# Gates of a graph-and-convolution GRU layer: Sigmoid written as Tanh of the half, and the state's part of the new gate halved by ScalarE in PSUM

## The chip, the cores and the metric

The kernel runs on one core of a Trainium2 chip. A core has five engines that run side by side, each with its own instruction stream: TensorE (PE, matmuls into PSUM), VectorE (DVE, elementwise work), ScalarE (ACT, activation functions), GpSimd (POOL) and SyncE (SP); DMA queues move data between the device memory and the on-chip memory SBUF. The metric is the device time of one launch in microseconds (us), given as the median of several executions. One further execution was recorded by the hardware profiler; its rows are what this document reads.

## The reference

For each of 32 batch items with 512 nodes and 256 channels, the layer normalises `x`, takes the positive part, and feeds a GRU cell with two inputs: a convolution branch and a sum over neighbours weighted by `exp(-dist) * adj`.

```python
h = jnp.maximum(_layernorm(x, axis=-1), 0.0)
# inside the layer, x is h:
x_conv = relu(bn2(conv1d_17(relu(bn1(conv1d_1(xT))))) + xT).T
A = jnp.exp(-dist) * mask                     # dist from a 3-wide projection of x
x_nmp = jnp.einsum('bnm,bmd->bnd', A, relu(x @ w_msg.T + b_msg))
gi = jnp.concatenate([x_conv, x_nmp], axis=-1) @ w_ih.T + b_ih
gh = x @ w_hh.T + b_hh
r = jax.nn.sigmoid(gi_r + gh_r)
z = jax.nn.sigmoid(gi_z + gh_z)
nn_ = jnp.tanh(gi_n + r * gh_n)
out = x_outer + (1.0 - z) * nn_ + z * x
```

All of it is in float32.

## The kernel before, in words

The program has five streams, each a Python generator: `rows` (first convolution, 1 tap), `begins` (normalising and turning the items), `graphs` (messages, distances, Exp, mask, neighbour sums), `conv` (the 17-tap convolution as a fast algorithm with 25 products in each of seven groups of items) and `gates` (the GRU). A planner at the end of the file picks the next piece of the stream that lags most. It keeps an estimate `now` of TensorE's time and estimates `free` of when VectorE and ScalarE will have done what they were given. Work that depends on another engine's result isn't issued at once: `later(t, f)` queues the function `f` for the estimated time `t`, and `fill()` issues what is due after each piece and then gives VectorE background work. So each engine has a fixed order in the built program, and a change of what is issued also shifts the plan of everything else. The estimates know a fixed cost and a cost per element for each instruction; they don't know loads of activation tables.

**The gates.** For each item `b` there are two halves `o` of 128 output channels. Each of the tiles below is 128 channels by 512 nodes and fills one PSUM bank. The tiles come in turn from the pool `acc`, which has two buffers (L98), so a tile takes the bank of the tile before last, and its first matmul waits until that one has been read.

- `ps_r` gets six matmuls: two from the state `hTb`, two from `xconv`, two from `xnb`. `reset` (L1088) settles everything that is queued and applies Sigmoid with the summed bias `brz`; the result is `r`.
- `ps_h` gets two matmuls from the state. For o = 0 they stand between the first two and the last four matmuls of `ps_r`; for o = 1 they follow `ps_r`; for the very last half they follow `ps_z`. `reset_hidden` (L1096) makes `r = (ps_h + b_hh) * r` on VectorE in one operation.
- `ps_z` gets six matmuls; `update` (L1102) makes `z` by Sigmoid.
- `ps_n` gets four matmuls from `xconv` and `xnb`. `mix` (L1108) adds `ps_n` to `r` on VectorE, `mix_next` (L1035) applies Tanh on ScalarE, `mix_last` (L1042) forms `n + z * (h - n)` with three VectorE operations, and `leave` turns the tile, adds the residual `res`, and has it stored by GpSimd's queue.
- For the very last half, `mix_ahead` (L1065) prepares `z * h` plus the residual and `1 - z` ahead of time, and `ps_n` is made in two slices of 384 and 128 nodes.

The bank order is ps_r, ps_h, ps_z, ps_n, again and again: ps_z waits for the activation that reads ps_r, and ps_n waits for reset_hidden, which reads ps_h.

**Other users of ScalarE.** `kernel_exp` (L861) applies Exp to four tiles for each item; Copy, Identity and Relu evacuate the products of the other streams (`mid`, `h`, `right`, `part`, `msg`). In the program built from this kernel an activation table is loaded at the start and then at each change from Sigmoid to Exp and back, 52 loads in all.

All the instructions that the planner records for VectorE and ScalarE carry the line of its helper (L127), and nearly all matmuls carry L136, so the rows of the profile are told apart by tile names.

Of the kernel before, what the change touches and what calls it, by code (L numbers as in the profile page):

```python
# [8 lines left out]
F32 = mybir.dt.float32  # L9
AF = mybir.ActivationFunctionType  # L10
ALU = mybir.AluOpType
PSUM = bass.MemoryType.PSUM

P = 128
# [10 lines left out]
_COL = {}  # L25
# [23 lines left out]
def kernel(  # L49
# [34 lines left out]
    ND = D // P  # L84
# [8 lines left out]
    const = ctx.enter_context(tc.tile_pool(name="const", bufs=1))  # L93
# [37 lines left out]
    dve, act = Engine(nc.vector, 0.12, 0.00108), Engine(nc.scalar, 0.16, 0.0009)  # L131

    def matmul(ps, lhsT, rhs, **more):
        nonlocal now
        now += max(0.223, 0.005 + elements(ps) / 600.0)
        nc.tensor.matmul(ps, lhsT, rhs, **more)  # L136
# [21 lines left out]
    def later(t, f):  # L158
        LATER.append((t, f))
        LATER.sort(key=lambda e: e[0])  # L160
# [59 lines left out]
    def load_gates(b):  # L220
        if b >= B or b in HB:
            return
        settle_stores()
        HB[b] = late.tile([P, ND, N], F32, name="hTb", bufs=2)
        nc.sync.dma_start(HB[b], HD[b])
# [29 lines left out]
    vec = const.tile([P, _NCOL], F32)  # L255
# [747 lines left out]
    def gates(b):  # L1003

        load_gates(b)
        load_sums(b, 0)
        load_sums(b, 1)
        if b == 0:
            yield now + 8.0
        hT = HB[b]  # L1010
        x_in = []

        def cols(o, g):
            return slice(g * D + o * P, g * D + (o + 1) * P)

        def products(ps, o, g, ks, then=None, of=None):


            sources = ((whh, 0), (wih, 0), (wih, ND))
            of = of or ks  # L1020
            for k in ks:
                w, at = sources[k]
                for i in range(ND):
                    matmul(
                        ps, w[:, at + i, cols(o, g)], hT[:, i, :] if k == 0 else x_in[2 * k - 2 + i],
                        start=(k == of[0] and i == 0), stop=(k == of[-1] and i == ND - 1),
                    )
                if k == ks[-1] and then is not None:
                    then()
                if k == 2 and o == ND - 1 and g == 2:  # L1030
                    load_sums(b + 1, 0)
                    load_sums(b + 1, 1)
                yield now

        def mix_next(r, z, o, s):  # L1035
            act.activation(
                r[:, s], r[:, s], AF.Tanh,
                bias=vec[:, _COL["b_ih"] + 2 * ND + o : _COL["b_ih"] + 2 * ND + o + 1],
            )
            later(act.free + 0.3, lambda: mix_last(r, z, o, s))  # L1040

        def mix_last(r, z, o, s):  # L1042
            y = XR[b, o]
            if is_last(o):
                dve.tensor_tensor(z[:, s], z[:, s], r[:, s], op=ALU.mult)
                dve.transpose(r[:, s], z[:, s])
                dve.tensor_tensor(y[:, s], r[:, s], y[:, s], op=ALU.add)
                later(dve.free + 0.4, lambda: store(y, o, s))
                return
            t = late.tile([P, N], F32, name="o_sb")  # L1050
            dve.tensor_tensor(t, hT[:, o, :], r, op=ALU.subtract)
            dve.tensor_tensor(t, z, t, op=ALU.mult)
            dve.tensor_tensor(r, r, t, op=ALU.add)
            later(dve.free, lambda: leave(r, t, y, o))

        def leave(r, t, y, o):

            dve.transpose(t, r)
            dve.tensor_tensor(y, t, y, op=ALU.add)
            later(dve.free + 0.4, lambda: store(y, o, slice(0, N)))  # L1060

        def is_last(o):
            return b == B - 1 and o == ND - 1

        def mix_ahead(z, o):  # L1065

            y = XR[b, o]
            zh, turned = (late.tile([P, Q * U], F32, name="part", bufs=3)[:, :N] for _ in range(2))
            dve.tensor_tensor(zh, z, hT[:, o, :], op=ALU.mult)
            dve.tensor_scalar(z, z, -1.0, 1.0, op0=ALU.mult, op1=ALU.add)  # L1070
            dve.transpose(turned, zh)
            dve.tensor_tensor(y, turned, y, op=ALU.add)

        def store(y, o, s):
            for g in range(P // 32):
                at = slice(32 * g, 32 * g + 32)
                queue = nc.gpsimd if s.stop - s.start == N else nc.scalar if g % 2 else nc.sync
                queue.dma_start(  # L1078
                    OB[b][:, s.start // 32 : s.stop // 32, o * P + 32 * g : o * P + 32 * g + 32],
                    y[at, s].rearrange("i (k j) -> i k j", j=32),  # L1080
                )
            if s.stop == N:
                del XR[b, o]

        for o in range(ND):
            r = z = None

            def reset():  # L1088
                nonlocal r
                settle()  # L1090
                if b == o == 0:
                    load_res(b, o)
                r = late.tile([P, N], F32, name="r", bufs=2)
                act.activation(r, ps_r, AF.Sigmoid, bias=brz[:, o : o + 1])

            def reset_hidden(ps_h):  # L1096
                dve.scalar_tensor_tensor(
                    r, ps_h, vec[:, _COL["b_hh"] + 2 * ND + o : _COL["b_hh"] + 2 * ND + o + 1], r,
                    op0=ALU.add, op1=ALU.mult,
                )  # L1100

            def update():  # L1102
                nonlocal z
                load_res(b + o, 1 - o)
                z = late.tile([P, N], F32, name="z")
                act.activation(z, ps_z, AF.Sigmoid, bias=brz[:, ND + o : ND + o + 1])

            def mix(s=slice(0, N)):  # L1108
                dve.tensor_tensor(r[:, s], ps_n[:, s], r[:, s], op=ALU.add)
                later(dve.free + 0.3, lambda r=r, z=z, o=o: mix_next(r, z, o, s))  # L1110

            ps_r = acc.tile([P, N], F32, name="ps_acc")
            ps_h = None
            yield from products(ps_r, o, 0, (0,), of=(0, 2))
            if o == 0:
                ps_h = acc.tile([P, N], F32, name="ps_acc")
                yield from products(ps_h, o, 2, (0,))
                if b not in XC:
                    yield lambda: b in evacuated
                    yield evacuated[b]  # L1120
                    load_conv(b)
                if b not in RES:
                    yield XC_AT[b]
                    residual(b)
                yield lambda: RES[b] < 1e9
                yield RES[b]
                x_in.extend([XC[b][:, i, :] for i in range(ND)] + [XN[b, d] for d in range(ND)])
            yield from products(ps_r, o, 0, (1, 2), reset, (0, 2))

            def hidden():  # L1130
                ps = acc.tile([P, N], F32, name="ps_acc")
                yield from products(ps, o, 2, (0,), lambda: reset_hidden(ps))

            if ps_h is not None:
                reset_hidden(ps_h)
            elif not is_last(o):
                yield from hidden()
            ps_z = acc.tile([P, N], F32, name="ps_acc")
            yield from products(ps_z, o, 1, (0, 1, 2), update)
            if is_last(o):  # L1140
                later(act.free + 0.2, lambda: mix_ahead(z, o))
                yield from hidden()
            if o == 0:
                load_gates(b + 1)
                load_conv(b + 1)
            else:
                residual(b + 1)
            ps_n = acc.tile([P, N], F32, name="ps_acc")
            if b < B - 1 or o < ND - 1:
                yield from products(ps_n, o, 2, (1, 2) if o == 0 else (2, 1), mix)  # L1150
                continue

            for s in (slice(0, N - P), slice(N - P, N)):
                if s.start > 0:
                    ps_n = acc.tile([P, N], F32, name="ps_acc")
                for j in range(2 * ND):
                    matmul(
                        ps_n[:, s], wih[:, j, cols(o, 2)], x_in[j][:, s],
                        start=(j == 0), stop=(j == 2 * ND - 1),
                    )  # L1160
                mix(s)
                yield now
            settle()
# [102 lines left out]
    while 0 in NORMS:  # L1266
# [5 lines left out]
    brz = const.tile([P, 2 * ND], F32)  # L1272
    dve.tensor_tensor(
        brz, vec[:, _COL["b_ih"] : _COL["b_ih"] + 2 * ND], vec[:, _COL["b_hh"] : _COL["b_hh"] + 2 * ND],
        op=ALU.add,
    )
    NORM_AT[0] = act.free + LAG
    load(1)
    spare = cv.tile([P, 9 * NZ], F32, name="y")
# [88 lines left out]
```

## Time and profile before

| | before |
|---|---|
| median of 8 runs | 2113.61 us (2109.25 to 2118.49) |
| profiled execution, own time | 2116.55 us |
| its span, first to last instruction | 2114.6 us |
| mean granted clock of TensorE | 0.993 |
| GpSimd (POOL) busy | 339.7 us, 16% |
| table loads on ScalarE | 52, together 66.7 us |
| Sigmoid of r, of z | 64 of 687 ns, 64 of 688 ns |
| Tanh of the new gate, 128x512 | 63 of 718 ns |
| first gate matmul | about 240 us into the span |
| only gate work left from | about 1891 us, 31.94 us for each item |

In a group's row, "x64 | 44.0, 688 | 234.8 <-PE ps_acc" means 64 instructions, 44.0 us busy in all, 688 ns each on average, and 234.8 us in which the engine was idle just before them, ended mostly by TensorE's work on ps_acc. A float32 matmul of 128x512 appears as two records; eight records back to back take 3.43 us. In a row of the timeline the first number is the start in us from the beginning of the span, the second the duration, and a bracket gives the idle time before it and what ended it. A row of busy time by stretch gives the stretch, its length, the busy time and number of instructions of the five columns PE, PEld (weight loads), DVE, ACT and POOL, and then TensorE's granted clock, the DMA share and GB/s.

### The profile page before, as it was taken

To read this page: it belongs to the slowest core of one execution; us is meant where nothing else is said; L and a number is where in the kernel's file an instruction comes from. 1 tells how busy PE (TensorE), PEld (TensorE's weight loads), DVE (VectorE), ACT (ScalarE), POOL (GpSimd) and SP (SyncE) were. 2 spreads that over 40 slices of the span, in tenths; PEclk is the share of its full clock that TensorE was granted. 3 is DMA by queue.
4 is the path that set the end of the run, shared out by engine and by line. 5 is a ranking of instruction groups with operands and counts; after the bars stand their busy time and mean duration, and the time that the engine had idled before them with its cause. 6 is when DMAs were issued, how large, how long until landed. Compare 5 with 4: busy or idle time off the path is not lost.

```text
span 2114.6 us, 25916 instructions
## 1 busy us (share of the span) xinstructions
PE 2060.5 (97%) x8774; PEld 1260.1 (60%) x8774; DVE 1512.8 (72%) x2660; ACT 754.5 (36%) x1267; POOL 339.7 (16%) x582
## 2 busy tenths in 40 slices
PE   9999899999999999999999999999999999999998
PEld 5887466665666556656466665456665666654443
DVE  6887488985988668877497865588985877753333
ACT  5543532236432253322443323533124432232111
POOL 2000112211201021111121101211111110112111
PEclk9999999999999999999999999999999999999999
DMA  7446787776866767666766777677766656624332
GB/s 275 164 143 204 254 249 199 194 212 173 236 209 191 220 180 198 182 186 189 220 182 173 189 203 186 188 184 207 211 180 191 188 153 168 169 72 108 86 90 40
DMA packets 546436, 383.07 MB, mean 181 GB/s; under 512 B 456576, under 2 KB 473472, under 8 KB 545664
## 3 DMA queue, kind: packets, MB, share of 16 engines
q1 hardware_dynamic: 512992, 282.17, 50.6%
q0 software_dynamic: 28624, 86.01, 12.0%
q10 hardware_dynamic: 4688, 13.24, 1.6%
q8 instruction: 70, 1.15, 0.2%
q14 instruction: 62, 0.51, 0.1%
HBM read 281.95 MB, written 99.35 MB: 180 GB/s over the span
## 4 chain that ended last, share of the span: by engine, by line
PE 61%; DMA 2%; DVE 1%; issue 1%; ACT 1%; SPq 1%; POOL 0%; DVEq 0%; POOLq 0%; ACTq 0%
PE ps_acc L136 36%; PE ps_g L136 11%; PE ps_c L136 9%; PE ps_b L136 4%; PE ps_b L867 1%; DMA m_sb<-in_adj_dram 1%; ACT r L127 1%; PE ps_g L141 0%; DMA hd<-hT 0%; SPq L339 0%; DMA hT<-hd 0%; DVE y L127 0%; DMA xnb<-nd 0%; DVE right L127 0%; DVE at L127 0%
## 5 line engine op out<-in xcount | busy, mean ns | idle before, releaser
L136 PE MATMUL ps_acc<-hTb,whh 128*128 128x512 f32 x768 | 358.8, 598 | 18.9 <-ACT r L127 15.1
L136 PE MATMUL ps_acc<-xconv,wih 128*128 128x512 f32 (+1 forms) x772 | 362.3, 592 | 0.1
L136 PE MATMUL ps_acc<-xnb,wih 128*128 128x512 f32 (+1 forms) x772 | 358.6, 591 | 2.6 <-DMA xnb<-nd 2.6
L136 PEld LDWEIGHTS ps_c<-xd,w 128*128 128x128 f32 x2400 | 294.1, 191 | 33.0 <-issue 29.2
L136 PE MATMUL ps_c<-xd,w 128*128 128x135 f32 (+1 forms) x2400 | 303.5, 279 | 2.1 <-issue 2.1
L1078 POOL DMA_DIRECT2D out_dram<-res x252 | 164.5, 659 | 617.8 <-DVE res L127 527.0
L136 PEld LDWEIGHTS ps_acc<-hTb,whh 128*128 128x128 f32 x768 | 140.2, 190 | 180.1 <-issue 136.9
L136 PEld LDWEIGHTS ps_acc<-xnb,wih 128*128 128x128 f32 x772 | 142.7, 190 | 160.3 <-issue 153.0
L136 PEld LDWEIGHTS ps_acc<-xconv,wih 128*128 128x128 f32 x772 | 142.8, 190 | 157.5 <-issue 154.2
L136 PE MATMUL ps_g<-at,msg 128*128 128x512 f32 x512 | 227.2, 593 | 1.5 <-DVE at L127 1.5
L136 PEld LDWEIGHTS ps_b<-x,w 128*128 128x128 f32 x1200 | 157.0, 190 | 43.7 <-issue 37.3
L127 ACT ACTIVATE mid<-ps_b 128x270 f32<-128x270 f32 (+1 forms) x150 | 59.5, 396 | 343.9 <-PE ps_b L136 333.3
L127 DVE TENSOR_TENSOR r<-ps_acc,r 128x512 f32<-128x512 f32 (+1 forms) x65 | 44.2, 682 | 191.0 <-PE ps_acc L136 190.9
L136 PE MATMUL ps_b<-x,w 128*128 128x135 f32 (+1 forms) x1200 | 163.1, 278 | 1.1 <-DVE xd L127 1.1
L136 PEld LDWEIGHTS ps_g<-at,msg 128*128 128x128 f32 x512 | 95.4, 190 | 112.4 <-issue 108.1
L127 DVE SCALAR_TENSOR_TENSOR x<-x,x 128x544 f32<-128x544 f32 (+5 forms) x161 | 137.7, 855 | 2.9
L136 PE MATMUL ps_g<-hT,w 128*128 128x512 f32 (+4 forms) x288 | 124.4, 580 | 13.6 <-DMA hT<-hd 9.6
L127 DVE TENSOR_TENSOR msg<-ps_g,bmsg 128x256 f32<-128x256 f32 x128 | 53.8, 421 | 108.6 <-PE ps_g L136 108.3
L127 ACT ACTIVATE z<-ps_acc,brz 128x512 f32<-128x512 f32 x64 | 44.0, 688 | 234.8 <-PE ps_acc L136 234.7
L127 DVE TENSOR_TENSOR x<-x 128x272 f32<-128x272 f32 (+5 forms) x280 | 127.6, 497 | 0.2
L127 DVE TENSOR_TENSOR xd<-x 128x544 f32<-128x544 f32 (+1 forms) x150 | 106.6, 718 | 25.0 <-PE ps_c L136 24.7
L136 PE MATMUL ps_g<-wmsg,hTg 128*128 128x259 f32 x496 | 124.1, 382 | 0.3 <-DVE aug L127 0.3
(121 smaller groups left out, 2593.8 us busy)
## 6 DMA issues: line engine op xcount, KB each, us to landing
w<-wd SPq DMA_DIRECT2D x125, 768.0 KB, 5.4
m_sb<-in_adj_dram SPq DMA_DIRECT2D x384, 64.0 KB, 3.3
hd<-hT POOLq DMA_DIRECT2D x32, 512.0 KB, 6.6
hT<-hd SPq DMA_DIRECT2D x32, 512.0 KB, 4.8
hTb<-hd SPq DMA_DIRECT2D x32, 512.0 KB, 5.5
xnb<-nd SPq DMA_DIRECT2D x64, 256.0 KB, 3.6
xconv<-cd SPq DMA_DIRECT2D x32, 512.0 KB, 5.5
res<-in_x_dram SPq DMA_DIRECT2D x256, 64.0 KB, 3.1
```

Of the source, the lines that this page charges most:

```text
L127: getattr(self.engine, name)(*tiles, **more)
L136: nc.tensor.matmul(ps, lhsT, rhs, **more)
L867: nc.tensor.matmul(pss[c], gr.left[k, :], gr.right[k, :], start=True, stop=True, tile_position=(32 * c, 0),)
L1078: queue.dma_start(OB[b][:, s.start // 32 : s.stop // 32, o * P + 32 * g : o * P + 32 * g + 32], y[at, s].rearrange("i (k j) -> i k j", j=32),)
```

## The change

The gates no longer use Sigmoid. With t = tanh(a / 2), the sigmoid of a is (t + 1) / 2. `reset` and `update` apply Tanh with scale 0.5 and a bias that was halved once at the start (one more VectorE operation on `brz`, and one that makes the halved `bn` from `b_hh`). The factors 1/2 and the additions of 1 go into the operations that use r and z:

- the state's part of the new gate is halved, with its bias, by a new ScalarE activation `hidden_half`, which reads the bank of ps_h and writes the result back to the same bank; `reset_hidden` is then `(t_r + 1) * half` and is no longer issued directly after the matmuls or the activation of r but queued by `reset_later` for 0.3 us after the estimated end of ScalarE's work (and made at the latest in `mix`);
- in `mix_last` two of the three operations become operations with a constant: `(t_z + 1) * (h - n)` and `0.5 * that + n`;
- `mix_ahead` gets the same treatment.

```diff
-            dve.tensor_tensor(t, z, t, op=ALU.mult)
-            dve.tensor_tensor(r, r, t, op=ALU.add)
+            dve.scalar_tensor_tensor(t, z, 1.0, t, op0=ALU.add, op1=ALU.mult)
+            dve.scalar_tensor_tensor(r, t, 0.5, r, op0=ALU.mult, op1=ALU.add)
...
-            dve.tensor_tensor(zh, z, hT[:, o, :], op=ALU.mult)
-            dve.tensor_scalar(z, z, -1.0, 1.0, op0=ALU.mult, op1=ALU.add)
+            dve.scalar_tensor_tensor(zh, z, 1.0, hT[:, o, :], op0=ALU.add, op1=ALU.mult)
+            dve.tensor_scalar(z, z, -0.5, 0.5, op0=ALU.mult, op1=ALU.add)
             dve.transpose(turned, zh)
-            dve.tensor_tensor(y, turned, y, op=ALU.add)
+            dve.scalar_tensor_tensor(y, turned, 0.5, y, op0=ALU.mult, op1=ALU.add)
...
-                act.activation(r, ps_r, AF.Sigmoid, bias=brz[:, o : o + 1])
-
-            def reset_hidden(ps_h):
-                dve.scalar_tensor_tensor(
-                    r, ps_h, vec[:, _COL["b_hh"] + 2 * ND + o : _COL["b_hh"] + 2 * ND + o + 1], r,
-                    op0=ALU.add, op1=ALU.mult,
-                )
+                act.activation(r, ps_r, AF.Tanh, bias=brz[:, o : o + 1], scale=0.5)
+
+            def hidden_half(ps_h):
+                act.activation(ps_h, ps_h, AF.Identity, bias=bn[:, o : o + 1], scale=0.5)
+
+            halves = []
+
+            def reset_hidden():
+                if halves:
+                    dve.scalar_tensor_tensor(r, r, 1.0, halves.pop(), op0=ALU.add, op1=ALU.mult)
+
+            def reset_later(ps_h):
+                halves.append(ps_h)
+                later(act.free + 0.3, reset_hidden)
...
-                act.activation(z, ps_z, AF.Sigmoid, bias=brz[:, ND + o : ND + o + 1])
+                act.activation(
+                    z, ps_z, AF.Tanh, bias=brz[:, ND + o : ND + o + 1], scale=0.5
+                )

             def mix(s=slice(0, N)):
+                reset_hidden()
...
-                yield from products(ps_h, o, 2, (0,))
+                yield from products(ps_h, o, 2, (0,), lambda: hidden_half(ps_h))
...
-                yield from products(ps, o, 2, (0,), lambda: reset_hidden(ps))
+                yield from products(ps, o, 2, (0,), lambda: hidden_half(ps))
+                reset_later(ps)

             if ps_h is not None:
-                reset_hidden(ps_h)
+                reset_later(ps_h)
...
+    dve.tensor_scalar(brz, brz, 0.5, None, op0=ALU.mult)
+    bn = const.tile([P, ND], F32)
+    dve.tensor_scalar(
+        bn, vec[:, _COL["b_hh"] + 2 * ND : _COL["b_hh"] + 3 * ND], 0.5, None, op0=ALU.mult
+    )
```

## The prediction

> **What bounds the kernel now.** I read the busy table first, then who waited for whom, then the gaps of TensorE in order of time, then the groups of ScalarE.
>
> ```profile
> PE 2060.5 (97%) x8774; PEld 1260.1 (60%) x8774; DVE 1512.8 (72%) x2660; ACT 754.5 (36%) x1267; POOL 339.7 (16%) x582
> PE 61%; DMA 2%; DVE 1%; issue 1%; ACT 1%; SPq 1%; POOL 0%; DVEq 0%; POOLq 0%; ACTq 0%
> ```
>
> TensorE is busy for 2060.5 of 2114.6 us and leads the chain of waits (which names ACT for 1%). Its matmuls don't change, so a gain can come only out of the 54.1 us in which it is idle, and out of stretches in which its clock is low. The waits of TensorE say what its idle time ends on (total us, times, longest):
>
> ```profile
> PE ps_acc L136 <- ACT r L127: 15.1, 17, 2.3
> PE ps_g L136 <- DMA hT<-hd: 9.6, 4, 5.2
> PE ps_acc L136 <- DVE r L127: 3.5, 3, 1.6
> PE ps_acc L136 <- DMA xnb<-nd: 2.6, 1, 2.6
> ```
>
> The largest is the one that the change touches: ps_z takes over the bank of ps_r and waits until ScalarE has read it. Of these 17 gaps, 14 are exactly 0.78 us, one is 0.23, and two are longer: 1.64 us (at 501.16) and 2.34 us (at 1346.35). 0.78 us is the activation of r itself; it is the whole gap in the last seven batches, where only gate work is left:
>
> ```profile
> 1984.52 1.88 PE L136 MATMUL ps_acc<-xnb,wih 128*128 128x512 f32 x4
> 1987.18 1.98 PE L136 MATMUL ps_acc<-hTb,whh 128*128 128x512 f32 x4 [0.78 <-ACT r L127]
> 1986.44 0.69 ACT L127 ACTIVATE r<-ps_acc,brz 128x512 f32<-128x512 f32 x1 [5.42 <-PE ps_acc L136]
> ```
>
> No table is loaded there, so nothing of this 0.78 can go. What a load can do is seen at the longest gap:
>
> ```profile
> 1340.94 1.28 ACT L127 ACT_TABLE_LOAD   x1
> 1342.23 0.60 ACT L127 ACTIVATE at<-ps_b 128x512 f32<-128x512 f32 x1
> 1342.73 1.57 ACT L127 ACTIVATE at<-ps_g 128x512 f32<-128x512 f32 x3
> 1344.32 1.28 ACT L127 ACT_TABLE_LOAD   x1
> 1345.61 0.69 ACT L127 ACTIVATE r<-ps_acc,brz 128x512 f32<-128x512 f32 x1
> ```
>
> ScalarE loads the table for Exp, does the four Exps, loads the table for Sigmoid, and only then reads ps_r, whose last matmul was over at 1344.0.
>
> **Table loads.** The trace and the order of instructions say how many there are:
>
> ```profile
> L127 ACT ACT_TABLE_LOAD x52 | 66.7, 1283 | 9.6 <-DMA x_sb<-in_x_dram 3.7 <-PE ps_acc L136 3.5 <-issue 1.6
> L127 ACT ACTIVATE z<-ps_acc,brz 128x512 f32<-128x512 f32 x64 | 44.0, 688 | 234.8 <-PE ps_acc L136 234.7
> L127 ACT ACTIVATE at<-ps_g 128x512 f32<-128x512 f32 x128 | 69.5, 602 | 89.2 <-PE ps_g L136 86.3 <-issue 2.6 <-PE ps_g L867 0.3
> ```
>
> In the changed program's order one load stands at the start and none after it, so Exp, Tanh and the simple functions do share one table: 51 x 1.283 = 65.4 us of ScalarE go. The Trainium skill (ScalarE: Activation LUTs, section What ACT_TABLE_LOAD costs) prices a switch at about 2.66 us, half of it a drain; by it 136 us would go. Here r begins at 1345.61, 1.29 after the load that began at 1344.32, so I take the row. On the path both give the same, since r can't begin before its ps_r.
>
> Where do loads lengthen the path? I held every load against the 46.6 us of gaps that TensorE's timeline names.
> - At 1346.35 (in the changed order the same matmuls and activations stand here, without both loads): 2.34 - 0.78 = **1.56 us**.
> - At 501.16 a load at 499.13 stands between an evacuation and r. In the changed order this r stands ahead of the Exps and has two conv1 products (3.4 us) behind it as cover: **1.64 us**.
> - At 492.41 (1.15 us, for at) the load ended at 490.98, before its ps_b at 491.27. No gain.
> - The other loads fall where ScalarE would be waiting anyway: r and z show 177 and 235 us of idle time for TensorE.
>
> The gap at 1346.35 also costs clock:
>
> ```profile
> 1348.00:1350.00 2.00, 2.00 (x4) 0.82 (x3) 1.90 (x4) 1.35 (x3) 0.93 (x2) 0.50 0.44 69
> ```
>
> (the third number from the end is the granted clock.) Over 1346 to 1352 the mean is 0.72: 6 x 0.28 = 1.7 us lost. The Trainium skill (TensorE: Matmul & The Clock Gate, Part 1) lets the clock fall only after an idle window of some 3.4 us; by that a gap of 2.34 us costs no clock and the sum is 3.2 us. The row shows a fall after a short gap that follows the small Exp products (5 rows of the array), so I take **1.7 us** as saved; the lower end is 0, as a gap of 0.78 remains. Sum of the loads: 1.56 + 1.64 + 1.7 = **4.9 us**, from 1.6 to 4.9.
>
> **Sigmoid to Tanh of the half.** 128 activations of the same shapes, operands and bias column: 687 and 688 ns today; Tanh on r from SBUF is 718. I take 688, so 0; at worst 0.03 on each of the roughly 15 naked gaps, 0.5 us.
>
> **hidden_half.** 64 new activations, PSUM to the same PSUM bank, with a bias column. No row writes PSUM from ScalarE. Ends: 602 (Exp from PSUM without bias) and 718; nearest by operands is z with 688. 64 x 0.688 = 44.0 us of ScalarE, less than the 65.4 that go. On the path: for o = 0 it runs right after ps_h, long before r. For o = 1 it stands behind r and ahead of z; queued behind it are mid, the Exps or z, and TensorE waits for mid and Exps for only 0.5 and 3.5 us in all. Cost 0; if all 64 were naked, 44. A rule speaks against it: the Trainium skill (ScalarE: Activation LUTs, Rules for kernel authors) gives adds and multiplies to VectorE. By it the step should stay where it was free, inside a VectorE operation of 746 ns. The busy table decides: VectorE 72% and up to 93% in a stretch of 100 us (600 to 700), ScalarE 29% there. I keep 0.
>
> **VectorE.** reset_hidden loses its bias column:
>
> ```profile
> L127 DVE SCALAR_TENSOR_TENSOR r<-ps_acc,vec,r 128x512 f32<-128x512 f32 x64 | 47.8, 746 | 74.7 <-PE ps_acc L136 44.1 <-ACT r L127 30.3
> L127 DVE TENSOR_TENSOR o_sb<-z,o_sb 128x512 f32<-128x512 f32 x63 | 43.6, 692 | 2.2
> L127 DVE SCALAR_TENSOR_TENSOR gg<-g,gg 128x512 f32<-128x512 f32 x12 | 8.1, 687 | 0.2
> ```
>
> With constants it should cost as the gg row, 687: 64 x 0.06 = 3.8 us less. The two mix operations (63 each) go from 692 to that form: 0. It is also issued later, so the 30.3 us in which VectorE stood before ScalarE's r become work on other things; that shortens VectorE's queue, with no gap that I can name for it. The two small operations at the start (172 ns rows) are 0.34 us, in a stretch where VectorE is 73% busy: 0, at most 0.34.
>
> **The added wait.** ps_n takes the bank of ps_h. Its chain was PE, VectorE; it is PE, ScalarE, VectorE: 0.2 + 0.69 + 0.1 + 0.69 = 1.7 us. The cover is at least the six matmuls of ps_z, 6 x 0.858 = 5.15 us, and by the order it is over 7 us ahead of the last seven batches. Behind the new operation on VectorE stand adds of the convolution and masks; the wait isn't long enough to reach TensorE. At the very end the reset now stands behind the four operations of mix_ahead (2.5 us from 2102.9), ending about 2106.3, just where the last slice's matmuls start today: 0, at most 0.1.
>
> **The moved order.** The planner gets 64 more activations, so streams shift. The order of TensorE is the same up to the ninth graph (about 300 us) and in its last 1379 instructions; it differs mostly in 300 to 760 and 985 to 1150. Six gaps lie there besides those of 0.78 and those counted (1.50, 2.56, 0.32, 1.64, 1.13, 2.44 = 9.6 us) and 1.7 us of low clock at 1042. New ones can take their place; I count 0, from -11.3 to +12.4 (below). Stores on POOL and loads on SP swap places in the same stretches.
>
> **Sum.** The profiled execution took 2116.55 us, span 2114.6 and 1.95 around it. 2116.55 - 4.9 = 2111.65. It lies 2.94 above the median of the eight runs (2113.61), so I predict **2108.7 us** for the median. What a measurement can tell from no change is about 0.2%, 4.2 us: under 2109.4 is faster, over 2117.8 slower.
>
> **Rivals.**
> - *Nothing is won:* new gaps eat the saved ones; 2113.6. For it: ScalarE is only 36% busy. Against: the gap at 1346 keeps its order. 10%.
> - *Less queue, fewer gaps:* the freed engines and the new order close all six gaps and the low clock at 1042: 11.3 more, 2097.4. For it: three of the six end on VectorE. Against: three end on DMA. 18%.
> - *The new order brings transfers late (the slower side):* place: conv1 at a group's start, hT's store on POOL followed by its load on SP. Price: 2.44 us of gap and 1.7 of clock, 4.1, as at 1042.66. Three more: 2108.7 + 12.4 = 2121.1. It decides where a load lands later than its row products stand in TensorE's order. 19%.
> - *Late reset:* the postponed reset gets behind three y additions (3 x 1.84 = 5.5 us, more than 7.0 - 1.7). Price 1.15 us each, the mean of today's three gaps for DVE r; if 12 of the 50 ahead of the tail miss: 2122.5. Against: covers are mostly longer. 6%.
> - That the loads remain is ruled out by the order.
>
> **How the numbers follow.** My forecast has 47%, with its own range 2105 to 2113; 0.6 of it is beyond 0.2%. Faster: 0.28 + 0.18 + 0.01 = 0.47; same: 0.19 + 0.08 = 0.27; slower: 0.26. The range 2098 to 2122 leaves out the lower part of the second rival and the upper parts of the last two, a fifth.
>
> **What would show it.** One table load of 1.28 us; ScalarE near 733 us; the new group near 690 ns with 64; reset near 690; the gap after the twenty-fourth set of Exps at 0.78 and the clock whole there; 31.94 us for each of the last seven batches, as now. Wrong if gaps for DVE r multiply, or if the gaps for hT grow.

## The result, and the profile after

The changed kernel takes **2104.03 us** (median of 11 runs, 2100.74 to 2109.36) against 2113.75 us (30 runs); the ratio is 0.9955, with a 95% interval of 0.9946 to 0.9964. So it is 9.7 us faster, where 4.9 were forecast. The profiled execution took 2105.19 us, with a span of 2103.4.

The busy row of the changed kernel, from its page:

```profile
PE 2058.3 (98%) x8776; PEld 1260.9 (60%) x8776; DVE 1509.1 (72%) x2662; ACT 731.5 (35%) x1280; POOL 335.9 (16%) x582
```

ScalarE has lost 23.0 us of work, VectorE 3.7; TensorE only 2.2. The groups of the changed kernel that answer to the forecast's rows (shape, count, busy time, mean ns of one, idle time before):

```profile
L127 ACT ACT_TABLE_LOAD x1 | 1.3, 1283 | 3.7 <-DMA x_sb<-in_x_dram 3.7
L127 ACT ACTIVATE ps_acc<-ps_acc,bn 128x512 f32<-128x512 f32 x64 | 42.4, 663 | 115.8 <-PE ps_acc L136 115.7
L127 DVE SCALAR_TENSOR_TENSOR r<-r,ps_acc 128x512 f32<-128x512 f32 x64 | 43.6, 681 | 51.7 <-ACT ps_acc L127 26.4 <-ACT r L127 25.1
L127 DVE SCALAR_TENSOR_TENSOR o_sb<-z,o_sb 128x512 f32<-128x512 f32 x63 | 43.6, 692 | 2.2
```

One load is left. The halving takes 663 ns, the reset 681 instead of 746, and the mix with a constant takes 692 as the one without did. The waits of TensorE in the changed kernel (total us, times, longest) show where the idle time went:

```profile
PE ps_acc L136 <- ACT r L127: 13.5, 18, 0.8
PE ps_g L136 <- DMA hT<-hd: 5.2, 1, 5.2
PE ps_g L136 <- ACT at L127: 4.0, 3, 1.7
...
PE ps_c L136 <- DVE n L127: 1.6, 1, 1.6
...
PE ps_acc L136 <- DVE r L127: 0.3, 1, 0.3
```

The longest wait for r is now 0.78 us, three of four waits for hT are gone (9.6 to 5.2 us; the one left lies before the gates begin), DVE r has fallen from 3.5 to 0.3, and the wait for xnb (2.6) is no longer there. The gaps of TensorE's timeline sum to 37.8 us, before to 46.6: 8.8 of the 11.1 us between the two spans. The place at 1346, first before, then in the changed kernel:

```profile
1346.35 3.38 PE L136 MATMUL ps_acc<-hTb,whh 128*128 128x512 f32 x4 [2.34 <-ACT r L127]
```

```profile
1334.31 1.59 ACT L127 ACTIVATE at<-ps_g 128x512 f32<-128x512 f32 x3
1335.05 1.98 PE L136 MATMUL ps_acc<-xnb,wih 128*128 128x512 f32 x4
1337.08 0.69 ACT L127 ACTIVATE r<-ps_acc,brz 128x512 f32<-128x512 f32 x1 [1.18 <-PE ps_acc L136]
1337.82 1.98 PE L136 MATMUL ps_acc<-hTb,whh 128*128 128x512 f32 x4 [0.78 <-ACT r L127]
```

Now ScalarE is idle for 1.18 us until ps_r is filled, where before ps_r lay ready while a table was loaded. The four matmul records behind the gap take 1.98 us where they took 3.38 at half clock.

**What a span is made of.** If from each profiled span the gaps of TensorE's timeline are taken, and what the granted clock cost (1 minus the clock, summed over the span), 2052.7 us are left for before (2114.55 - 46.59 - 15.24) and 2052.7 for the changed kernel (2103.42 - 37.82 - 12.89). So differences between these two have to be looked for in gaps and in the clock. The span and the mean clock are recorded for the single runs too, and their means even out how the clock happened to fall in one execution. Lost to the clock is span x (1 - clock); the rest holds the gaps and the work. e1 to e4 ran on one chip and e5 to e8 on another, each beside runs of the kernel before. The ratio is the one on record, which can differ a little from that of the medians:

| kernel | runs | median us | ratio, 95% interval | lost to the clock, mean | rest of the span, mean |
|---|---|---|---|---|---|
| before, beside e1 to e4 | 29 | 2113.07 | | 14.7 | 2096.5 |
| before, beside e5 to e8 | 17 | 2114.22 | | 16.0 | 2096.0 |
| changed | 11 | 2104.03 | 0.9955 (0.9946 to 0.9964) | 12.6 | 2089.7 |
| e1: old order, no loads | 11 | 2109.65 | 0.9983 (0.9975 to 0.9992) | 13.8 | 2094.0 |
| e2: change in the old order | 11 | 2115.54 | 1.0009 (0.9997 to 1.0020) | 17.7 | 2095.6 |
| e3: new order with loads | 11 | 2112.46 | 0.9995 (0.9986 to 1.0004) | 17.3 | 2093.2 |
| e4: a second activation | 6 | 2105.33 | 0.9965 (0.9951 to 0.9979) | 12.6 | 2091.4 |
| e5: e2, reset put off | 11 | 2110.99 | 0.9989 (0.9979 to 1.0000) | 14.2 | 2095.4 |
| e6: changed, reset at once | 5 | 2105.72 | 0.9962 (0.9949 to 0.9975) | 13.0 | 2090.0 |
| e7: changed, again | 6 | 2104.96 | 0.9964 (0.9951 to 0.9977) | 13.3 | 2090.7 |
| e8: ps_h as cover | 4 | 2085.38 | 0.9869 (0.9854 to 0.9884) | 8.9 | 2075.3 |

The standard error of the mean is 0.3 to 0.8 us in the last column (1.1 for e8), and 0.5 to 1.3 us for the clock.

### The profile page after: what moved, and what is told of

Same layout as the page of the kernel before. It is cut to its first block, busy times and chain, and to the rows that moved or that the text cites. A ratio compares the mean times of both kernels' runs of the same rounds, so it can differ in the third digit from the quotient of the medians.

```text
span 2103.4 us, 25938 instructions
## 1 busy us (share of the span) xinstructions
PE 2058.3 (98%) x8776; PEld 1260.9 (60%) x8776; DVE 1509.1 (72%) x2662; ACT 731.5 (35%) x1280; POOL 335.9 (16%) x582
## 3 DMA queue, kind: packets, MB, share of 16 engines
q1 hardware_dynamic: 512992, 282.17, 51.5%
q8 instruction: 70, 1.15, 0.2%
## 4 chain that ended last, share of the span: by engine, by line
PE 92%; DVE 4%; ACT 2%; issue 1%; DMA 1%; POOL 0%; ACTq 0%; DVEq 0%
PE ps_acc L136 47%; PE ps_g L136 20%; PE ps_c L136 15%; PE ps_b L136 6%; PE ps_g L141 1%; PE ps_b L867 1%; ACT r L127 1%; DVE at L127 1%; DVE gg L127 1%; DVE z L127 1%; DVE x L127 1%; DVE y L127 0%; PE ps_acc L146 0%; ACT y L127 0%; ACT at L127 0%
```

## The experiments

The theory: the loads cost 4.9 us on the path, as forecast, and the other 4.8 come from the shifted order. The rivals: the loads were worth all of it, by ways that I hadn't named (queue), or the order was (order).

### e1 and e3: loads and order, each alone

e1 is the kernel before with another function name, e3 the changed kernel with the old one. e1 leaves out the halves around Tanh and e3 takes Sigmoid of half the sum, so neither computes the layer's gates; only their times are read.

```diff
e1, from before:
-                act.activation(r, ps_r, AF.Sigmoid, bias=brz[:, o : o + 1])
+                act.activation(r, ps_r, AF.Tanh, bias=brz[:, o : o + 1])
...
-                act.activation(z, ps_z, AF.Sigmoid, bias=brz[:, ND + o : ND + o + 1])
+                act.activation(z, ps_z, AF.Tanh, bias=brz[:, ND + o : ND + o + 1])
e3, from the changed kernel, for r and likewise for z:
-                act.activation(r, ps_r, AF.Tanh, bias=brz[:, o : o + 1], scale=0.5)
+                act.activation(r, ps_r, AF.Sigmoid, bias=brz[:, o : o + 1], scale=0.5)
```

> The kernel before with Tanh in the place of Sigmoid for r and z and nothing else (so r and z are tanh(a), not the sigmoid); every engine's order is that of before, without 51 table loads. Loads theory (the loads cost 4.9 us on TensorE's path, at 501.16, at 1346.35 and in the clock behind it; the rest of the measured 9.7 us comes from the new order): 4.9 us less than before, ratio 0.9977. Queue theory (the loads slow ScalarE and with it VectorE in many places that I didn't name, and the order gives nothing): 9.7 us less, ratio 0.9954. Order theory (the loads were hidden, the new order gives all): 0 to 1.5 us less, ratio 0.9993 to 1.0.

> The changed kernel with Sigmoid in the place of Tanh for r and z (so r and z are sigmoid(a/2) and the gates are not the reference's); every engine's order is that of the changed kernel, with the table loads back (52 in all). Loads theory with a gain from the order: about 4.8 us less than before, ratio 0.9977. Queue theory: as before, ratio 1.0. Order theory: 8 to 9.7 us less, ratio 0.9955 to 0.9962.

Measured: 2109.65 us (0.9983) and 2112.46 us (0.9995). Without the loads the old order gains 3.4 us, and the waits for r fall by just what was named for that order, from 15.1 to 12.7 us: by 0.86 at 501 and 1.56 at 1346.

```profile
PE ps_acc L136 <- ACT r L127: 12.7, 17, 0.8
```

The new order with the loads (and with the halving) gains 0.6 us, which its interval doesn't tell from nothing. **No theory is right as it stands**: 3.4 and 0.6 don't add up to 9.7. In the new order the loads are worth 6.5 to 8.5 us (ratio 0.9995 against 0.9955 and, in e7, 0.9964), and without the loads the new order is worth 4 to 6 (0.9983 against the same two). This second figure takes the new order together with the change's arithmetic, which e1 doesn't have; e2 and e5 below have it in the old order. Loads and order aren't independent: a load costs more where the new order has put it. e3 shows how. This is its timeline at an Exp block that is followed by conv1:

```profile
489.00 0.69 ACT L127 ACTIVATE r<-ps_acc,brz 128x512 f32<-128x512 f32 x1 [2.07 <-PE ps_acc L136]
489.59 1.08 ACT L127 ACTIVATE x_sb<-x_sb,shift,rstd 128x256 f32<-128x256 f32 x2
490.69 1.28 ACT L127 ACT_TABLE_LOAD   x1
491.98 0.60 ACT L127 ACTIVATE at<-ps_b 128x512 f32<-128x512 f32 x1
492.48 1.57 ACT L127 ACTIVATE at<-ps_g 128x512 f32<-128x512 f32 x3
493.12 4.54 PE L136 MATMUL ps_g<-hT,w 128*128 128x512 f32 x6 [3.08 <-ACT at L127]
```

and the same place in the changed kernel:

```profile
487.60 0.69 ACT L127 ACTIVATE r<-ps_acc,brz 128x512 f32<-128x512 f32 x1 [2.06 <-PE ps_acc L136]
488.19 1.08 ACT L127 ACTIVATE x_sb<-x_sb,shift,rstd 128x256 f32<-128x256 f32 x2
489.17 0.58 ACT L127 ACTIVATE at<-ps_b 128x512 f32<-128x512 f32 x1
489.65 1.56 ACT L127 ACTIVATE at<-ps_g 128x512 f32<-128x512 f32 x3
490.29 4.11 PE L136 MATMUL ps_g<-hT,w 128*128 128x512 f32 x5 [1.65 <-ACT at L127]
```

The new order puts r ahead of the Exps, and conv1 waits for the first Exp to free a bank. With a load between them the gap is 3.08 us, without 1.65. In e3 such waits for `at` are 1.4 us longer here, 0.9 at 535 and 0.9 at 748. These 3.2 us are about the difference in the rest of the span (2093.2 and 2089.7); the larger part, 4.7 us, is lost to the clock (17.3 us a run, not 12.6), and what ties it to these waits isn't shown. In the old order the load stood before the Exps too, but no r did, and the load was over before TensorE had filled ps_b:

```profile
489.70 1.28 ACT L127 ACT_TABLE_LOAD   x1
491.27 0.60 ACT L127 ACTIVATE at<-ps_b 128x512 f32<-128x512 f32 x1 [0.28 <-PE ps_g L867]
```

### e2 and e5: the arithmetic of the change in the old order

e2 has the change's operations, but the halving and the two operations at the start are issued past the planner, so that TensorE's, GpSimd's and SyncE's orders are those of before. e5 puts the reset off:

```diff
e2, from before (with Tanh and the mix of the change):
+            def hidden_half(ps_h):
+                nc.scalar.activation(ps_h, ps_h, AF.Identity, bias=bn[:, o : o + 1], scale=0.5)
...
+                yield from products(ps, o, 2, (0,), lambda: (hidden_half(ps), reset_hidden(ps)))
e5, from e2, inside reset_hidden:
-                dve.scalar_tensor_tensor(r, r, 1.0, ps_h, op0=ALU.add, op1=ALU.mult)
+                dve.free = max(dve.free, now) + dve.fixed + dve.each * N
+                halves.append(ps_h)
+                later(max(act.free, now) + 0.9, put)
```

`put` issues the same operation past the planner, and `mix` calls it as well.

> The whole change in its arithmetic, but in the order of before: the halving in PSUM and the two small operations at the start are put in without the planner's knowledge, and the reset stands directly behind the halving. Against e1 this adds 64 activations (42 us of ScalarE) and one more engine in the chain of the reset. If the halving is hidden, as predicted: the same as e1 within 1 us. If it is naked in places (rival): 3 to 10 us over e1, with gaps of TensorE that end on ScalarE's or VectorE's work for ps_acc. Order theory: 0 to 1.5 us less than before, since the order is that of before.

> As e2 (the change's arithmetic in the order of before), only that the reset on VectorE is put off by 0.9 us in the planner's time instead of standing directly behind the halving; all the other instructions keep their order. In e2 VectorE stood 60.4 us before resets for ScalarE's halving, in the changed kernel 26.4. If the blocked VectorE is what e2 lost against e1 (about 6 us): back to 2109 to 2111, ratio 0.998 to 0.999. If the halving on ScalarE itself, or a lower clock, costs it: as e2, 2114 to 2116, ratio 1.0005 to 1.001.

Measured: 2115.54 us (1.0009) and 2110.99 us (0.9989); e1 was 2109.65. So the change's arithmetic in the old order gains nothing, and with the reset put off (19 of 64 resets stand later on VectorE, by 1 to 6 places) most of e1's gain is back. In e2's profile VectorE waited before resets 60.4 us for the halving, in e5's 41.1:

```profile
L127 DVE SCALAR_TENSOR_TENSOR r<-r,ps_acc 128x512 f32<-128x512 f32 x64 | 43.7, 683 | 89.4 <-ACT ps_acc L1100 60.4 <-ACT r L127 28.8
L1105 DVE SCALAR_TENSOR_TENSOR r<-r,ps_acc 128x512 f32<-128x512 f32 x64 | 43.6, 682 | 64.0 <-ACT ps_acc L1108 41.1 <-ACT r L127 22.4
```

But the reading isn't as simple as expected: in the rest of the span e2 and e5 are alike (2095.6 and 2095.4, some 1.5 us over e1), and what sets them apart is the clock, 17.7 and 14.2 us with errors of 1.2 and 1.1. In both the waits for xnb and for DVE r are longer than in e1 (together 7.3 and 7.4 us of gaps, e1 5.6), which fits the 1.5 us: here the halving seems not to be free, though 1.5 us is only some two standard errors. Whether the blocked VectorE also brings the clock down, or the clock fell by chance, stays open; a repeat of e1 and e2 side by side wasn't made. With the change's arithmetic in both orders, the new order is worth 9.5 to 11.5 us against e2 and 5 to 7 against e5 (ratios 1.0009 and 0.9989 against 0.9955 and 0.9964), so what the order gives depends on what stands in it.

### e4 and e6: the halving and the postponed reset in the new order

```diff
e4, from the changed kernel:
                 act.activation(ps_h, ps_h, AF.Identity, bias=bn[:, o : o + 1], scale=0.5)
+                nc.scalar.activation(ps_h, ps_h, AF.Identity, bias=zero, scale=1.0)
e6, from the changed kernel (the planner's account of the reset stays where it was):
                 halves.append(ps_h)
+                nc.vector.scalar_tensor_tensor(r, r, 1.0, ps_h, op0=ALU.add, op1=ALU.mult)
```

> The changed kernel with a second activation on ps_h behind the halving, a copy onto itself (scale 1, bias 0), unknown to the planner: the order is that of the changed kernel, ScalarE has 64 more activations, 42 us. If the halving is hidden: at most 1 us more than the changed kernel (2104 to 2105, ratio 0.9955 to 0.996). If such an activation costs time on the path: 3 us more or above, ratio 0.997 or above.

> The changed kernel with the reset standing directly behind the halving on VectorE, all the other instructions in the order of the changed kernel. If the postponed reset matters: 3 to 6 us over the changed kernel, 2107 to 2110, ratio 0.997 to 0.9985, and VectorE stands some 60 us before resets. If not: as the changed kernel, ratio 0.9955.

e4: 2105.33 us, where the changed kernel gave 2104.03 and 2104.96. 42.4 us more of ScalarE's work cost 0.4 to 1.3 us, which the intervals don't tell from nothing: in the new order such an activation is hidden. e6: 2105.72 us, as the changed kernel. The expected 60 us of waiting weren't there (56.0, the changed kernel 51.5): by the order only 7 of the 64 resets stand elsewhere, by 2 to 4 places, as the changed kernel's `later` had let nearly all of them go at once. So e6 tells little of a reset that really comes late.

### e7: the changed kernel again

> The changed kernel once more, beside the others on the same chip. Ratio 0.9946 to 0.9964 as measured before. For the clock: if the stretches at half clock depend on chance as well as on the gaps, its profile shows them in other places, and other numbers of them, than the first profile of the same kernel (six stretches, 11.9 us lost), with gaps of TensorE that stay within 1 us of the 37.9 of the first.

2104.96 us, 0.9964 (0.9951 to 0.9977). The gaps of its profile are 39.3 us, not quite within the 1 us expected; behind 240 us they are 25.6 and 25.2, and what differs lies ahead of the gates. The stretches at half clock were other ones: about 28, 224, 232, 264, 488 and 740 us and the last 1.9 us in the first profile (12.9 us lost), about 28, 232, 268 and 740 and the last 5 us in the second (12.8). The gap ahead of conv1 behind the same Exps (1.65 us at 490.29 in the first, 1.66 at 491.81 in the second) had a fall of the clock behind it the first time and none the second. The records of the clock say more: within a profile all falls start a whole number of 3.41 us steps apart, so each step of 3.41 us can be looked at by itself. These are the steps around the gap, first of the first profile, then of the second:

```profile
487.04:490.45 3.41, 1.76 (x11) 0.48 (x10) 3.32 (x4) 2.85 (x6) 0.00 (x0) 1.00 0.00 0
490.45:493.86 3.41, 3.41 (x5) 1.35 (x6) 3.17 (x6) 0.76 (x2) 0.00 (x0) 0.50 0.66 104
```

```profile
486.68:490.09 3.41, 3.41 (x14) 1.07 (x12) 3.41 (x4) 1.35 (x3) 0.00 (x0) 1.00 0.29 117
490.09:493.51 3.42, 1.76 (x8) 0.87 (x5) 3.19 (x5) 2.64 (x6) 0.00 (x0) 1.00 0.20 31
493.51:496.92 3.41, 3.41 (x9) 1.52 (x8) 3.17 (x6) 3.09 (x8) 0.56 (x1) 1.00 0.82 125
```

TensorE was busy for 1.76 us in both steps that hold the gap. In the first profile 1.1 us of that were the Exp products of 5 rows, so that full matmuls filled 0.20 of the step, and the clock fell. In the second the Exp products lay in the step ahead, full matmuls filled 0.70 and 0.50 of the two steps, and it did not.

### e8: the state's part as cover for r

The largest wait left was the 0.78 us for r where ps_z follows ps_r directly. For o = 1 the two matmuls of ps_h stand between; for o = 0 they stood ahead, to have work while the convolution input is awaited. Where that input is ready, this isn't needed:

```diff
+                early = RES.get(b, 1e9) > now
+                if early:
-                ps_h = acc.tile([P, N], F32, name="ps_acc")
-                yield from products(ps_h, o, 2, (0,), lambda: hidden_half(ps_h))
+                    ps_h = acc.tile([P, N], F32, name="ps_acc")
+                    yield from products(ps_h, o, 2, (0,), lambda: hidden_half(ps_h))
```

> The changed kernel with one more edit: for o = 0 the state's part ps_h comes after ps_r, as for o = 1, when the item's convolution input is ready by then. Its two matmuls (1.7 us) then stand between ps_r and ps_z and cover the activation of r. By the order, places where ps_z follows ps_r directly fall from 21 to 4. If 0.78 us is lost at each: 16 x 0.78 = 12.5 us, the last batches at 31.17 instead of 31.94 us each, 2104 - 12 = 2092, ratio 0.990. Rival: new waits take its place (ps_n then has its bank's reset only 5.15 us ahead of it, and the streams shift): 2100 to 2106, ratio 0.9935 to 0.9965.

Measured: **2085.38 us**, 0.9869 (0.9854 to 0.9884) of before, some 19 us under the changed kernel, and so better than either and than expected. Its waits of TensorE:

```profile
PE ps_g L136 <- DMA hT<-hd: 7.0, 1, 7.0
PE ps_g L136 <- ACT at L127: 4.0, 3, 1.7
PE ps_acc L136 <- ACT r L127: 3.1, 4, 0.8
```

Four waits for r are left of 18. Its last batches:

```profile
2001.35 3.60 PE L136 MATMUL ps_acc<-hTb,whh 128*128 128x512 f32 x8
2004.79 1.88 PE L136 MATMUL ps_acc<-xconv,wih 128*128 128x512 f32 x4
2006.50 3.60 PE L136 MATMUL ps_acc<-xnb,wih 128*128 128x512 f32 x8
...
2032.25 3.60 PE L136 MATMUL ps_acc<-hTb,whh 128*128 128x512 f32 x8
```

The same row comes back after 30.90 us (2032.25 - 2001.35), where before and the changed kernel have 31.94. A wait that the timeline shows as 0.78 us costs **1.04 us**. The starts of single matmul records say where the rest is: in a series they lie 0.43 us apart, around a wait 1.37 and then 0.53, together 1.04 more. Each record is 0.59 us long and overlaps the next, so the idle time between two records is less than the delay. 14 waits fewer make 14.6 us, and the rest of the span fell by 14.4 to 15.4 (2089.7 and 2090.7 to 2075.3). The remaining 4 us are a smaller loss to the clock (8.9 instead of 12.6 and 13.3, over four runs only). The same edit on the kernel before wasn't measured.

## Why the prediction was right, and where it was too small

- **What bounds it.** Right: TensorE's work stayed, and all of the gain is in its gaps and its clock. Of the 11.1 us between the profiled spans 8.8 are gaps and 2.3 clock.
- **Table loads, 4.9 us.** Right in mechanism for the gaps and roughly in size. 51 went, and the gaps at 501 and 1346 went as said (3.2 us); taken as a single cause, in the old order, e1 measures 3.4 us (its interval reaches from 1.7 to 5.3). The old order keeps 0.78 us at 501, so 4.1 were due there. That the clock stayed whole at 1346, the other 1.7 us, was at least in part luck: in e2, e3, e4 and e5 the wait for r is 0.78 us there as well, and the clock fell all the same, at 1344.74, 1340.63, 1338.51 and 1340.66, each time ahead of that wait and behind the small Exp products. What the statement "the other loads fall where ScalarE would be waiting anyway" missed is that this depends on the order: in the new one three loads would lie ahead of Exps that TensorE waits for, and the loads would be worth 6.5 to 8.5 us.
- **Tanh for Sigmoid, 0.** Right: 687 and 688 ns as before.
- **hidden_half, 0.** Right for the changed order (e4); the duration was 663, not 688 ns. In the old order it probably cost some 1.5 us in gaps (e1 to e5).
- **VectorE.** Right: 681 for 687, 692 for 692, together 3.7 us less for the 3.8 forecast. Its waiting ahead of resets fell from 74.7 to 51.7 us, but not as said: of the 30.3 us for r 25.1 are left, and in place of 44.1 for TensorE's ps_h there are 26.4 for the halving.
- **The added wait.** Right: DVE r has one gap of 0.34 us, and the end of the kernel runs as worked out; the last reset is over at 2094.96, 0.2 us before the last slice's matmuls.
- **The moved order, counted as 0.** This is the term that was mis-sized. Of the six gaps named there (9.6 us) five closed and 0.34 us is left of that at 700; new ones in these stretches (0.67, 1.58, 0.44, 0.70, 0.55, 0.79) make 4.7, and there are two more waits of 0.78 for r. So these stretches gained some 3 us in the profile. A further 2.8 us went at 265 to 275, at 479 and at 1387, but only the 0.53 at 479 can be put down to the order: at 265 to 275 the profiles in the old order show 0.7 to 3.2 us and those in the new 0.7 to 2.5, and at 1387 the old order has 0 to 0.9. Over the runs, with the loads gone, order and arithmetic together gave about 5 us (e1 against the changed kernel), less than half of the rival "less queue, fewer gaps", and no transfer came late. e3 shows that this gain is real only without the loads.
- **Clock.** A loss of 1.7 us was set on one place, and the runs don't bear that out (see the loads). Over the runs the whole loss fell from 14.7 and 16.0 to 12.6 and 13.3.

The forecast 2108.7 us lay 4.7 us above the median. The direction was right, and the median lies within 2098 to 2122, but 1 us below the range given to the forecast's own mechanism (2105 to 2113): half of the gain came from the order, for which nothing was counted.

## What to carry to other kernels

Where TensorE is near full, count the places where it stands and name what ended each wait; busy time of another engine says little by itself (in e4 42 us more of it cost 0.4 to 1.3 us). In a kernel whose order a planner makes, an edit and the order that it brings aren't two terms to be added: measure the edit in the old order and the old code in the new order, as here (3.4 and 0.6 us alone, 9.7 together). And when a short wait comes back at the same place in each period, look for work already in the program to put in between: moving two matmuls was worth twice the change itself.

## What the runs showed of the hardware

- In all ten profiles the granted clock is 1.00 or 0.50. Within a profile its falls start whole numbers of 3.41 us apart (before: 57, 60, 72, 136, 297, 386 and 610 steps behind the first, at 29.25 us), and where the span doesn't end, each lasts one step or two; a step costs 1.7 us.
- A fall comes behind a step that is poor in full matmuls. From 236 to 2070 us the ten profiles have 31 falls: 29 follow a step of which matmuls of 128 rows filled at most 0.38, two a step with 0.42 and 0.49, and every step with less than 0.39 was followed by half clock. So a gap of 1.15 us beside the Exp products of 5 rows can bring a fall or none, as it lies to the steps; the ends of the matmuls are modelled, so the shares are rough.
- The clock makes much of the spread of runs of one kernel: in 29 runs of before the spread was 7.5 us (2109.69 to 2117.14), with 14.7 us lost to the clock on average (the correlation of loss and time over these runs is 0.61, with a clock that is recorded to 0.001, or 2.1 us).
- ScalarE writes PSUM in 663 ns (Identity, 128x512, bias column, from PSUM), where Tanh of the same shape and operands to SBUF takes 688. Copy and Exp from PSUM to SBUF without a bias column take 598 and 602, so the function hardly counts.
- A wait of 0.78 us between two series of matmuls lengthened the period by 1.04 us.
